# Halves in the sums behind the experts, Gelu read straight from PSUM banks, and a reordered first scan chunk

## The chip, the cores and the metric

The kernel runs on one core of one Trainium2 chip. The metric is the device time of one execution in microseconds; the value given is the median of several. Everything is float32. TensorE (PE) multiplies matrices into PSUM (eight banks of 512 columns); VectorE (DVE), ScalarE (ACT) and GpSimd (POOL) do the elementwise work; SyncE (SP) issues nearly all DMAs. GpSimd has no operand in PSUM in this kernel. Each engine takes its instructions strictly in the order in which they stand in its queue.

## The reference, cut to what matters

Input x is (4, 384, 32, 32): four batches, 384 channels, 1024 positions. Two layers follow each other, each with a mixer and a feed-forward part, both with a residual.

```python
# layer 0
x = x + L0_conv(_ln_c(x))      # selective scan over 4 directions, then layer norm and gelu
t = _to_tokens(x)              # (batch, 1024 tokens, 384)
t = t + L0_ffn(_ln_t(t))       # mixture of 4 experts, the best 2 of each token
# layer 1
x = x + L1_conv(_ln_c(x))      # attention, 8 heads of 64, one projection for q, k and v
t = t + L1_ffn(_ln_t(t))       # 384 -> 1536 -> 384 by Kronecker products, gelu between
```

```python
def step(h, inp):                                   # L0_conv, state of 16 per channel
    dA = jnp.exp(dtt[..., None] * A)
    h = h * dA + (dtt * ut)[..., None] * bt[:, :, None, :]
    y = jnp.einsum('bkdn,bkn->bkd', h, ct)
# dt = softplus(projection + bias)
# L0_ffn
h = gelu(einsum('bsd,edh->ebsh', x, w1) + b1); y = einsum('ebsh,ehd->ebsd', h, w2) + b2
out = einsum('bse,ebsd->bsd', masked, y)            # masked: renormed weights of the best two
# L1_ffn
h = gelu(x @ kron(c_fc_1, c_fc_2).T); out = h @ kron(c_proj_1, c_proj_2).T
```

## The kernel before

**The scan layer** (`scan_layer`, L186) goes through 32 units: 4 batches, 4 directions, 2 halves of 512 positions. A unit is prepared by `project` (L297), a generator that is advanced while the unit before it is scanned; the first unit has nothing before it and is prepared at once. `project` makes dt = softplus(p + bias) for three chunks of 128 channels: `begin` (L363) runs six ACT steps (Abs, Relu, Exp, +1, Ln, and 1 minus or minus 1), and the four terms ln(1+e), -e', e' and relu are then added up. For batch 0 this is done by TensorE, four products with the identity (L378, two records each); for the later batches by two GpSimd subtractions (L395, L396) and one VectorE addition (L402). Then du = dt * u is made by VectorE (L403) and dt copied by ACT (L404), and both go to DRAM (`dd`, L405, L406).

`chunk` (L409) loads dt and du back, spread over partitions as (state, channel): for each of q = 0, 1 a tile of dt (s = 0) and one of du (s = 1), each by four DMAs (L424). For each of four state groups and each q, GpSimd multiplies du by B (L440, 128x1024), ACT makes exp(A dt) (L449), VectorE scans (L454), the result is multiplied by C (GpSimd L468 for q = 0, VectorE L461 for q = 1), and TensorE adds over the states (L475).

**The tail** of a batch is put in behind the scan of the next batch and runs beside it: `route` (gates, places, rows scattered by GpSimd's indirect DMAs), `experts`, `combine`, `prologue`, `attention`, `last_layers`. The tail of the last batch, and what is left of the one before it, runs alone.

`experts` (L893) goes through 11 slots, 8 of 256 rows and 3 of 128. Per slot: TensorE fills a bank with hidden tiles (L963), ACT brings them to SBUF adding the bias (L968, Identity), and when all 12 tiles are there one wide Gelu is done in place (L971); then TensorE makes y (L978). Gelu and Exp/Ln are in different activation tables; `exp_again` (L145) loads the Exp table back at once (L148).

`combine` (L989) gathers each token's two rows by 16 indirect DMAs (L1008), adds them weighted on TensorE for each of eight blocks of 128 tokens (L1015), and VectorE adds the residual (L1018); the sum goes to DRAM in one DMA (L1019). `prologue` (L1024) then takes mean and variance of all eight blocks (`stats`, L536), the inverse root (Ln, Exp on ACT), -mean/std by `less_mean` (L548, through a "p" bank), normalises eight blocks on ACT (L1031), and transposes them to channels (L1039, copies L1043), first half before second.

`attention` (L1046) projects (L1064), transposes (L1073), and for each step multiplies scores (L1087), takes Exp (L1093) and multiplies with v (L1133).

`last_layers` (L1146) computes, for each half i, the output projection and residual (L1185, L1187), mean, variance and z (L1196 to L1216), and then the feed-forward part: `hidden` (L1224) makes six hidden tiles, two at a time: two matmuls of 32 rows (L1231), two ACT copies (L1237), and after the sixth one wide Gelu of 128x3072 (L1240) and the Exp table back. Six matmuls of 32 columns add them to f_acc (L1248). After two such groups f_acc is copied (L1253), multiplied out (L1256), added to the residual (L1258) and stored (L1259).

**Banks and buffers.** `Room` hands out tiles by tag. Beside the scan the tail has one bank "o" and three banks "p" (NARROW_BANKS); from the attention of the last batch on it has two and six (WIDE_BANKS), as the scan's banks are free.

**The order** on every queue is written when the program is built: a planner simulates the program with its own estimates of durations (`schedule_with_timeline_sim=True`, L1389) and lets each engine take the ready instruction of highest priority. Earlier emission is higher priority; `high_priority(offset=FORWARD)` moves combine, prologue and last_layers forward, and `issue_after` and `depend` tie one instruction behind another. A change in one place can so change the order elsewhere.

Of the kernel before, what the change touches and what calls it, by code (L numbers as in the profile page):

```python
# [9 lines left out]
F32 = mybir.dt.float32  # L10
I32 = mybir.dt.int32
AF = mybir.ActivationFunctionType
# [5 lines left out]
P = 128  # L18
B = 4
D = 384  # L20
DC = D // P
HW = 32
L = HW * HW
HF = 512
NH = L // HF
# [12 lines left out]
FC = HID // P  # L38
# [7 lines left out]
NSLOT = NFULL + NHALF  # L46
# [5 lines left out]
MB = L // P  # L52
# [6 lines left out]
KR = 32  # L59
# [24 lines left out]
EXACT = {"kw": 4, "k12": 2, "k4": 4, "got": 2}  # L84

FORWARD = 20000

NARROW_BANKS = {"o": 1, "p": 3}
WIDE_BANKS = {"o": 2, "p": 6}
# [26 lines left out]
class Body:  # L116
# [69 lines left out]
    def scan_layer(self, x1, between):  # L186

        nc, tc, a = self.nc, self.tc, self.a
        with ExitStack() as ctx:
# [4 lines left out]
            psum = ctx.enter_context(tc.tile_pool(name="s_ps", bufs=2, space=PSUM))  # L194
# [31 lines left out]
            def finish(b, y, i):  # L226
# [19 lines left out]
                for k in ORDER  # L246
                for i in (range(NH) if k < 2 else reversed(range(NH)))
            ]
            us = {0: start(0)}
            ahead = []  # L250
            self.place_behind = None
# [6 lines left out]
            for n, unit in enumerate(units):  # L258
                b, k, i = unit
# [37 lines left out]
    def project(self, unit, u, wx, work, dram, psum, made):  # L297
# [25 lines left out]
        def k2(name, shape=(P, HF)):  # L323
            return work.tile([*shape], F32, tag="k2", name=name, bufs=6)
# [35 lines left out]
        made += [bcs, dd]  # L360
        yield

        def begin(c):  # L363
            ps = psum.tile([P, HF], F32, tag="ps", name="dt_ps")
            nc.tensor.matmul(ps, wdt[:, c * P : (c + 1) * P], xd, start=True, stop=True)  # L365
            bias = self.col("dtb", k * DC + c)
            mag, one_e, lnw = k2("mag"), k2("one_e"), k2("lnw")
            relu = k2("relu") if b == 0 else ps
            nc.scalar.activation(mag, ps, AF.Abs, bias=bias)
            nc.scalar.activation(relu, ps, AF.Relu, bias=bias)  # L370
            nc.scalar.activation(mag, mag, AF.Exp, scale=-1.0)
# [11 lines left out]
            return ps, mag, one_e, lnw  # L383

        def behind(engine):
            if self.place_behind is None:
# [1 line left out]
            return self.tc.issue_after(self.place_behind[engine])  # L388

        for c in range(DC):  # L390
            ps, mag, one_e, lnw = begin(c)
            yield
            if b > 0:
                with behind("pool"):
                    nc.gpsimd.tensor_sub(mag, one_e, mag)  # L395
                    nc.gpsimd.tensor_sub(lnw, lnw, mag)  # L396
            yield
            d, du = mag, one_e
            rows = slice(c * P, (c + 1) * P)
            with behind("dve"):  # L400
                if b > 0:
                    nc.vector.tensor_add(ps, ps, lnw)  # L402
                nc.vector.tensor_mul(split(du), split(ps), part(c))  # L403
            nc.scalar.copy(d, ps)  # L404
            nc.sync.dma_start(out=dd[0, rows, :], in_=d)  # L405
            ins = nc.sync.dma_start(out=dd[1, rows, :], in_=du).ins  # L406
        made.append(ins)

    def chunk(self, unit, first, c, fed, carry, nega, sel, acc, work, dap):  # L409
# [6 lines left out]
        dtr = []  # L416
        for q in range(NJ // 2):

            pair = []
            at = c * P + q * 2 * DB  # L420
            for s in range(2):
                t = work.tile([P, 2, HF], F32, tag="dtr", name="dtr", bufs=7)
                for n in range(NJ):
                    nc.sync.dma_start(  # L424
                        out=t[n * DB : (n + 1) * DB],
                        in_=dd[s, at : at + 2 * DB, :].rearrange("(j d) l -> d j l", d=DB),
                    )
                pair.append(t)
            dtr.append(pair)

        def run(ap):
# [74 lines left out]
    def first_layer(self, b, room):  # L506

        self.experts(b, self.slots, room)
        with self.tc.high_priority(offset=FORWARD):
            xt, xn = self.combine(b, *self.place, room)  # L510
            return self.prologue(xt, xn, room)

    def second_layer(self, b, xc, room, between):
        att = self.attention(xc, self.sums[:, b], room)
# [18 lines left out]

        return self.x2[b].rearrange("(m p) d -> p m d", p=P)

    def stats(self, xt, eps, room):  # L536

        nc = self.nc
        st = room.tile([P, MB, 6], "st", "st")
        mv = room.tile([P, MB, 2], "mv", "mv")  # L540
        rstd = room.tile([P, MB], "rstd", "rstd")
        for m in range(MB):
            nc.vector.bn_stats(st[:, m, :], xt[:, m, :])
            nc.vector.bn_aggr(mv[:, m, :], st[:, m, :])
        self.inverse_root(rstd, mv[:, :, 1], eps)
        return mv[:, :, 0], rstd

    def less_mean(self, mean, rstd, room, tag):  # L548

        less = room.tile([P, MB], tag, "less")  # L550
        ps = room.bank("p", "less_ps")[:, :MB]
        self.nc.scalar.copy(ps, rstd)
        self.nc.vector.scalar_tensor_tensor(less, mean, -1.0, ps, op0=ALU.mult, op1=ALU.mult)
        return less
# [338 lines left out]
    def experts(self, b, routed, room):  # L893
# [60 lines left out]
        for s in range(NSLOT):  # L954
            w1, w2, bb = weights
            at, size = extent(s)
            hs = room.tile([P, FC, size], "k12", "hs")
            n = HF // size
            for f in range(0, FC, n):
                ps = room.bank("p", "h_ps").rearrange("p (r l) -> p r l", l=size)  # L960
                for r in range(n):
                    for c in range(DC):
                        nc.tensor.matmul(  # L963
                            ps[:, r, :], w1[(f + r) // wf][:, c, (f + r) % wf * P : ((f + r) % wf + 1) * P],
                            xc[:, c, :], start=(c == 0), stop=(c == DC - 1),
                        )
                for r in range(n):
                    nc.scalar.activation(  # L968
                        hs[:, f + r, :], ps[:, r, :], AF.Identity, bias=bb[:, f + r : f + r + 1]
                    )  # L970
            self.exp_again(nc.scalar.activation(hs, hs, AF.Gelu).ins)  # L971
# [12 lines left out]
            queue = nc.sync if s + 1 < NSLOT else nc.scalar  # L984
            queue.dma_start(
                out=made[at : at + size, :].rearrange("(t p) d -> p t d", p=P), in_=y
            )

    def combine(self, b, pos, gate, room):  # L989
# [22 lines left out]
        for m in range(MB):  # L1012
            ps = room.bank("p", "w_ps")[:, :D]
            for k in range(TOP):
                nc.tensor.matmul(  # L1015
                    ps, diag[k][:, m, :], got[m][:, k, :], start=(k == 0), stop=(k == TOP - 1)
                )
            nc.vector.tensor_add(xt[:, m, :], xt[:, m, :], ps)  # L1018
        nc.sync.dma_start(out=self.tokens(b), in_=xt)  # L1019
        return xt, [got[m][:, 0, :] for m in range(MB)]  # L1020

    def prologue(self, xt, xn, room):  # L1024


        nc = self.nc
        mean, rstd = self.stats(xt, self.eps6, room)
        less = self.less_mean(mean, rstd, room, "less")
        for m in range(MB):  # L1030
            nc.scalar.activation(  # L1031
                xn[m], xt[:, m, :], AF.Identity, bias=less[:, m : m + 1], scale=rstd[:, m : m + 1]
            )
        xc = room.tile([P, DC, L], "k12", "xc")
# [111 lines left out]
    def last_layers(self, b, att, room, between=()):  # L1146
# [72 lines left out]

        for step in between:  # L1220
            step()
        ng = 6

        def hidden(i, at):  # L1224
            hs = room.tile([P, ng, HF], "k12", "hs")
            early = None
            for f in range(at, at + ng, 2):
# [269 lines left out]
```

## Time and profile before

| what | value |
|---|---|
| median of 3 runs (lowest, highest) | 4267.21 us (4253.81, 4271.01) |
| the profiled execution | 4260.96 us |
| its span, first to last instruction | 4258.3 us |
| busy: PE, POOL, DVE, ACT | 3330.8, 3020.0, 2838.3, 2519.7 us |
| granted TensorE clock, mean | 0.873 of full |

Where the time lies: the first product of the scan on GpSimd starts at 44.08 us; the first experts at 864; the scan's last accumulation ends at about 3426. The last batch's experts end at 3939, its gathers and sums at 3968, its attention at 4143, and its last output leaves VectorE at 4251.69.

How to read it: a line of the order of time gives start, length, engine, line, operation, output and inputs, shape and count; in brackets stands how long the engine was idle before it and what released it. Consecutive instructions of one kind are merged into one line, whose length then reaches from the first start to the last end. A float32 matmul appears as two records. A list of waits gives who waited, for whom, us in all, times, the longest. "Granted clock" is the share of TensorE's full clock that the throttle allowed.

### The profile page before, as it was taken

What the parts mean: (1) busy time and instruction counts of PE and PEld (TensorE: products, weight loads), DVE (VectorE), ACT (ScalarE), POOL (GpSimd) and SP (SyncE); (2) the same over time, 40 slices, a digit from 0 to 9 for tenths busy, and PEclk for the clock granted to TensorE, in tenths of its full rate; (3) what the DMA queues carried; (4) which work ended last, traced back from release to release, by engine and by line L of the source; (5) the groups of instructions that cost most, each with busy time, mean ns of one, the idle gap of its engine ahead of it and who ended that gap; (6) DMA issues with size and microseconds to landing.
All of it is one profiled execution on the core that took longest, in us unless ns stands there. A gap on an engine that the chain in (4) does not pass through costs nothing. (4 is left out here: it accounts for less than half of the span.)

```text
span 4258.3 us, 45670 instructions
## 1 busy us (share of the span) xinstructions
PE 3330.8 (78%) x13308; PEld 1572.8 (37%) x13308; DVE 2838.3 (67%) x4148; ACT 2519.7 (59%) x4486; POOL 3020.0 (71%) x1471
## 2 busy tenths in 40 slices
PE   6445544389887888689996888679986899998896
PEld 2111101155553223255552223245553235666222
DVE  5999997788877877788877878778877830000101
ACT  5555545566665876666665776667664763443454
POOL 5999998898888977889989888879988830000100
PEclk8766666699998999699998999689997999999997
DMA  5554464678786534668887434668788343345100
GB/s 140 126 129 122 124 172 110 204 204 233 228 257 162 152 107 136 192 204 230 232 258 210 124 100 133 192 183 235 225 250 230 93 152 110 121 150 191 50 26 20
DMA packets 410322, 693.70 MB, mean 163 GB/s; under 512 B 51024, under 2 KB 209616, under 8 KB 410064
## 3 DMA queue, kind: packets, MB, share of 16 engines
q1 hardware_dynamic: 400752, 664.29, 54.3%
q0 software_dynamic: 8192, 25.17, 1.8%
q8 instruction: 107, 1.75, 0.2%
q14 instruction: 151, 1.24, 0.1%
q10 hardware_dynamic: 1120, 1.25, 0.1%
HBM read 569.00 MB, written 121.50 MB: 162 GB/s over the span
## 5 line engine op out<-in xcount | busy, mean ns | idle before, releaser
L440 POOL TENSOR_TENSOR bx<-dtr,bcs 128x1024 f32<-128x1024 f32 x768 | 1793.7, 2362 | 195.6 <-PE acc L475 84.0
L449 ACT ACTIVATE da<-dtr,nega 128x512 f32<-128x512 f32 x1536 | 1045.9, 690 | 898.8 <-DVE bx L461 551.1
L468 POOL TENSOR_TENSOR bx<-bx,bcs 128x1024 f32<-128x1024 f32 x384 | 905.4, 2362 | 132.4 <-DVE carry L465 59.9
L475 PE MATMUL acc<-bx,sel 128*32 128x512 f32 x3072 | 488.0, 691 | 309.8 <-POOL bx L468 282.2
L963 PE MATMUL h_ps<-xc,w 128*128 128x256 f32 (+1 forms) x3168 | 666.6, 365 | 65.6 <-DVE xc L950 28.3
L978 PE MATMUL y_ps<-w,hs 128*128 128x384 f32 x1824 | 643.7, 506 | 55.9 <-ACT hs L971 54.9
L963 PEld LDWEIGHTS h_ps<-xc,w 128*128 128x128 f32 x3168 | 551.9, 198 | 241.3 <-issue 124.5
L454 DVE TENSOR_TENSOR_SCAN bx<-da,carry,bx 128x512 f32<-128x512 f32 x384 | 473.7, 1271 | 134.5 <-POOL bx L440 69.5
L454 DVE TENSOR_TENSOR_SCAN bx<-da,bx 128x512 f32<-128x512 f32 x384 | 452.3, 1210 | 125.4 <-POOL bx L440 69.7
L454 DVE TENSOR_TENSOR_SCAN da<-da,carry,bx 128x512 f32<-128x512 f32 x384 | 475.7, 1274 | 79.5 <-ACT da L449 63.1
L461 DVE TENSOR_TENSOR bx<-da,bcs 128x512 f32<-128x512 f32 x768 | 509.6, 681 | 2.9
L454 DVE TENSOR_TENSOR_SCAN da<-da,bx 128x512 f32<-128x512 f32 x384 | 455.4, 1219 | 67.5 <-ACT da L449 46.8
L978 PEld LDWEIGHTS y_ps<-w,hs 128*128 128x128 f32 x1824 | 353.1, 197 | 338.5 <-issue 68.7
L1093 ACT ACTIVATE ex<-s_ps 128x512 f32<-128x512 f32 x512 | 300.2, 591 | 128.7 <-PE s_ps L1087 126.8
L1087 PE MATMUL s_ps<-w 64*128 64x512 f32 x1024 | 302.6, 653 | 70.1 <-ACT ex L1093 68.4
L968 ACT ACTIVATE hs<-h_ps,bb 128x256 f32<-128x256 f32 (+1 forms) x528 | 199.4, 441 | 220.0 <-PE h_ps L963 216.4
L999 POOL TENSOR_TENSOR diag<-ident,g_weight 128x1024 f32<-128x1024 f32 x8 | 15.0, 1898 | 419.9 <-PE xc_ps L946 406.4
L1133 PE MATMUL o_acc<-ex,vt 128*64 128x512 f32 x1024 | 281.9, 629 | 18.3 <-ACT ex L1093 14.7
L475 PEld LDWEIGHTS acc<-bx,sel 128*32 128x32 f32 x3072 | 75.0, 115 | 597.1 <-POOL bx L468 392.5
L982 DVE TENSOR_TENSOR y<-y_ps,bb 128x384 f32<-128x384 f32 x76 | 41.8, 550 | 223.4 <-PE y_ps L978 223.2
L1087 PEld LDWEIGHTS s_ps<-w 64*128 64x128 f32 x1024 | 80.6, 187 | 271.4 <-ACT ex L1093 222.7
L365 PE MATMUL dt_ps<-xd,wdt 108*128 108x512 f32 x192 | 123.7, 731 | 69.6 <-ACT mag L404 37.0
(213 smaller groups left out, 3611.4 us busy)
## 6 DMA issues: line engine op xcount, KB each, us to landing
w<-in_w SPq DMA_DIRECT2D x352, 576.0 KB
dtr<-dd SPq DMA_DIRECT2D x1536, 128.0 KB
bcs<-both SPq DMA_DIRECT2D x512, 128.0 KB
dd<-one_e SPq DMA_DIRECT2D x96, 256.0 KB
dd<-mag SPq DMA_DIRECT2D x96, 256.0 KB
rows<-zero SPq DMA_DIRECT2D x76, 192.0 KB
xt<-x SPq DMA_DIRECT2D x32, 384.0 KB
xs<-rows SPq DMA_DIRECT2D x32, 384.0 KB
```

Source lines behind the costliest of these rows:

```text
L440: pool = nc.gpsimd.tensor_mul(bx, dtr[q][1], bc[:, 0].unsqueeze(1).to_broadcast([P, 2, HF])).ins
L449: nc.scalar.activation(da, dtr[q][0][:, j, :], AF.Exp, scale=nega[:, col : col + 1])
L454: nc.vector.tensor_tensor_scan(run(h), run(da), run(bx[:, j, :]), 0.0 if first else hold, ALU.mult, ALU.add,)
L461: dve = nc.vector.tensor_mul(bx[:, j, :], h, cg).ins
L468: pool = nc.gpsimd.tensor_mul(bx, bx, cg.unsqueeze(1).to_broadcast([P, 2, HF])).ins
L475: nc.tensor.matmul(acc[lo : lo + DB, :], sel, out[q][:, j, :], start=(g == 0), stop=(g == NG - 1),)
L963: nc.tensor.matmul(ps[:, r, :], w1[(f + r) // wf][:, c, (f + r) % wf * P : ((f + r) % wf + 1) * P], xc[:, c, :], start=(c == 0), stop=(c = ...
L968: nc.scalar.activation(hs[:, f + r, :], ps[:, r, :], AF.Identity, bias=bb[:, f + r : f + r + 1])
L978: nc.tensor.matmul(out[:, :D], hs[:, f, t * P : (t + 1) * P], w2[f // wf][:, f % wf, :], start=(f == 0), stop=(f == FC - 1),)
L1087: ins = nc.tensor.matmul(ps, w[rows, j * P : (j + 1) * P], w[rows, halves(i)], start=True, stop=True).ins
L1093: done.append(nc.scalar.activation(ex[:, o, :], ps, AF.Exp, scale=HD**-0.5, accum_out=sums[:, t, 2 * j + o, i : i + 1],).ins)
L1133: ins = nc.tensor.matmul(out[cols, :], made[t][1][:, j, cols], ex[:, o, :], start=(j == 0), stop=(j == MB - 1),).ins
```

## The change

Seven edits, in the order of the program:

1. Five (`WARM = 5`) matmuls of `ones` with itself (128x512) stand ahead of the first unit; nobody reads their result.
2. In the first unit, for its first chunk alone, dt is added up by GpSimd and VectorE, as in later batches, instead of by TensorE; Relu then stays in the bank.
3. For that chunk `chunk` loads du's tile ahead of dt's.
4. In the last slot of `experts` (128 rows, three banks of four tiles) the first eight tiles get one wide Gelu, tied behind the first matmul of the last tile; the last four tiles get Gelu with the bias straight from the bank.
5. The sums of `combine` become a function that `prologue` calls block by block; the store to DRAM goes in two halves.
6. `prologue` does statistics, inverse root, normalisation and transposes half by half; the "less" value goes through an "o" bank.
7. In the last batch `hidden` is replaced by `quickly`: four hidden tiles in four "p" banks, four Gelus straight from the banks, no copy, no `exp_again`; three such groups of four for each half instead of two of six.

```diff
+            warm = psum.tile([P, HF], F32, tag="ps", name="warm")
+            for _ in range(WARM):
+                nc.tensor.matmul(warm, self.ones, self.ones.unsqueeze(1).to_broadcast([P, HF // P, P]),
+                    start=True, stop=True)
             us = {0: start(0)}
...
+        alone = len(self.kept) == 1
         def begin(c):
+            by_products = b == 0 and not (alone and c == 0)
...
-            relu = k2("relu") if b == 0 else ps
+            relu = k2("relu") if by_products else ps
...
-            if b == 0:
+            if by_products:
...
-            if b > 0:
+            if not by_products:
                 with behind("pool"):
                     nc.gpsimd.tensor_sub(mag, one_e, mag)
...
-            for s in range(2):
+            for s in (1, 0) if unit == (0, 0, 0) and c == 0 else (0, 1):
```

```diff
             for f in range(0, FC, n):
+                last = s == NSLOT - 1 and f == FC - n
...
+                        if last and r == n - 1 and c == 0:
+                            wide = nc.scalar.activation(hs[:, :f, :], hs[:, :f, :], AF.Gelu).ins
+                            self.depend(wide, ins)
                 for r in range(n):
-                    nc.scalar.activation(
-                        hs[:, f + r, :], ps[:, r, :], AF.Identity, bias=bb[:, f + r : f + r + 1]
-                    )
-            self.exp_again(nc.scalar.activation(hs, hs, AF.Gelu).ins)
+                    done = nc.scalar.activation(
+                        hs[:, f + r, :], ps[:, r, :], AF.Gelu if last else AF.Identity,
+                        bias=bb[:, f + r : f + r + 1],
+                    ).ins
+            if not last:
+                done = nc.scalar.activation(hs, hs, AF.Gelu).ins
+            self.exp_again(done)
```

```diff
-        for m in range(MB):
+        def add(m):
...
-        nc.sync.dma_start(out=self.tokens(b), in_=xt)
+            if m % (MB // NH) == MB // NH - 1:
+                part = slice(m + 1 - MB // NH, m + 1)
+                nc.sync.dma_start(out=self.tokens(b)[:, part, :], in_=xt[:, part, :])
...
         for i in range(NH):
+            for j in range(nh):
+                m = i * nh + j
+                add(m)
+                nc.vector.bn_stats(st[:, j, :], xt[:, m, :])
+                nc.vector.bn_aggr(mv[:, j, :], st[:, j, :])
+            self.inverse_root(rstd, mv[:, :, 1], self.eps6)
+            less = self.less_mean(mv[:, :, 0], rstd, room, f"less{i}", "o")
+            for j in range(nh):
+                m = i * nh + j
+                nc.scalar.activation(
+                    xn[m], xt[:, m, :], AF.Identity, bias=less[:, j : j + 1], scale=rstd[:, j : j + 1]
+                )
             for c in range(DC):
                 ps = room.bank("p", "tc_ps")
```

```diff
-        ng = 6
+        alone = room.banks is WIDE_BANKS
+        ng = nq if alone else 6
+        def quickly(i, at):
+            hs = room.tile([P, ng, HF], "k12", "hs")
+            banks = [room.bank("p", "h_ps") for _ in range(nq)]
+            for o, ps in enumerate(banks):
+                rows = slice(o * KR, (o + 1) * KR)
+                nc.tensor.matmul(ps, fc1[rows, at // nq, :], zs[i][rows, :], start=True, stop=True)
+            for o, ps in enumerate(banks):
+                nc.scalar.activation(hs[:, o, :], ps, AF.Gelu)
+            return hs
```

More of the change, by code (lines that the diff above doesn't have):

```diff
@@ L86 @@
 FORWARD = 20000
+WARM = 5
 NARROW_BANKS = {"o": 1, "p": 3}
@@ L248, in scan_layer @@
             ]
+            warm = psum.tile([P, HF], F32, tag="ps", name="warm")
+            for _ in range(WARM):
+                nc.tensor.matmul(
+                    warm, self.ones, self.ones.unsqueeze(1).to_broadcast([P, HF // P, P]),
+                    start=True, stop=True,
+                )
             us = {0: start(0)}
@@ L382, in begin @@
                 nc.scalar.activation(one_e, one_e, AF.Identity, bias=self.minus1)
-            return ps, mag, one_e, lnw
+            return by_products, ps, mag, one_e, lnw
         def behind(engine):
@@ L390, in project @@
         for c in range(DC):
-            ps, mag, one_e, lnw = begin(c)
+            by_products, ps, mag, one_e, lnw = begin(c)
             yield
-            if b > 0:
+            if not by_products:
                 with behind("pool"):
@@ L400, in project @@
             with behind("dve"):
-                if b > 0:
+                if not by_products:
                     nc.vector.tensor_add(ps, ps, lnw)
@@ L417, in chunk @@
         for q in range(NJ // 2):
-            pair = []
+            pair = [None, None]
             at = c * P + q * 2 * DB
-            for s in range(2):
+            for s in (1, 0) if unit == (0, 0, 0) and c == 0 else (0, 1):
                 t = work.tile([P, 2, HF], F32, tag="dtr", name="dtr", bufs=7)
@@ L427, in chunk @@
                     )
-                pair.append(t)
+                pair[s] = t
             dtr.append(pair)
@@ L509, in first_layer @@
         with self.tc.high_priority(offset=FORWARD):
-            xt, xn = self.combine(b, *self.place, room)
-            return self.prologue(xt, xn, room)
+            xt, xn, add = self.combine(b, *self.place, room)
+            return self.prologue(xt, xn, room, add)
     def second_layer(self, b, xc, room, between):
@@ L534, in tokens, with less_mean @@
         return self.x2[b].rearrange("(m p) d -> p m d", p=P)
[L536 to L541, printed above, removed]
-        for m in range(MB):
[L543 to L551, printed above, removed]
+    def less_mean(self, mean, rstd, room, tag, bank="p"):
+        n = rstd.shape[-1]
+        less = room.tile([P, n], tag, "less")
+        ps = room.bank(bank, "less_ps")[:, :n]
         self.nc.scalar.copy(ps, rstd)
@@ L962, in experts @@
                     for c in range(DC):
[L963 removed]
+                        ins = nc.tensor.matmul(
                             ps[:, r, :], w1[(f + r) // wf][:, c, (f + r) % wf * P : ((f + r) % wf + 1) * P],
                             xc[:, c, :], start=(c == 0), stop=(c == DC - 1),
[L966 removed]
+                        ).ins
+                        if last and r == n - 1 and c == 0:
+                            wide = nc.scalar.activation(hs[:, :f, :], hs[:, :f, :], AF.Gelu).ins
+                            self.depend(wide, ins)
                 for r in range(n):
[L968 to L971 removed]
+                    done = nc.scalar.activation(
+                        hs[:, f + r, :], ps[:, r, :], AF.Gelu if last else AF.Identity,
+                        bias=bb[:, f + r : f + r + 1],
+                    ).ins
+            if not last:
+                done = nc.scalar.activation(hs, hs, AF.Gelu).ins
+            self.exp_again(done)
             if s + 1 < NSLOT:
@@ L1011, in combine @@
                 )
-        for m in range(MB):
+        def add(m):
             ps = room.bank("p", "w_ps")[:, :D]
@@ L1018, in combine, with prologue @@
             nc.vector.tensor_add(xt[:, m, :], xt[:, m, :], ps)
-        nc.sync.dma_start(out=self.tokens(b), in_=xt)
-        return xt, [got[m][:, 0, :] for m in range(MB)]
-    def prologue(self, xt, xn, room):
-        nc = self.nc
[L1028 to L1034, printed above, removed]
-        for i in range(NH):
+            if m % (MB // NH) == MB // NH - 1:
+                part = slice(m + 1 - MB // NH, m + 1)
+                nc.sync.dma_start(out=self.tokens(b)[:, part, :], in_=xt[:, part, :])
+        return xt, [got[m][:, 0, :] for m in range(MB)], add
+    def prologue(self, xt, xn, room, add=lambda m: None):
+        nc = self.nc
+        nh = MB // NH
+        xc = None
+        for i in range(NH):
+            st = room.tile([P, nh, 6], f"st{i}", "st")
+            mv = room.tile([P, nh, 2], f"mv{i}", "mv")
+            rstd = room.tile([P, nh], f"rstd{i}", "rstd")
+            for j in range(nh):
[9 more added lines that the diff above has]
+                    xn[m], xt[:, m, :], AF.Identity, bias=less[:, j : j + 1], scale=rstd[:, j : j + 1]
+                )
+            if xc is None:
+                xc = room.tile([P, DC, L], "k12", "xc")
             for c in range(DC):
@@ L1221, in last_layers @@
             step()
-        ng = 6
+        alone = room.banks is WIDE_BANKS
[5 more added lines that the diff above has]
+                rows = slice(o * KR, (o + 1) * KR)
+                nc.tensor.matmul(
+                    ps, fc1[rows, at // nq, :], zs[i][rows, :], start=True, stop=True
+                )
+            for o, ps in enumerate(banks):
+                nc.scalar.activation(hs[:, o, :], ps, AF.Gelu)
+            return hs
         def hidden(i, at):
+            if alone:
+                return quickly(i, at)
             hs = room.tile([P, ng, HF], "k12", "hs")
```

## The prediction

> **What bounds it now.** I read the table of stages first (busy time of each engine between two times; columns: stretch, its length, busy us and count for PE, PEld, DVE, ACT, POOL, then the granted TensorE clock, DMA share, GB/s).
>
> ```profile
> 44.00:864.00 820.00, 392.95 (x1234) 111.59 (x1234) 719.32 (x1034) 433.22 (x677) 775.00 (x353) 0.67 0.53 141
> 864.00:3428.00 2564.00, 2157.19 (x8989) 1065.65 (x8989) 2025.24 (x2876) 1707.07 (x3035) 2205.05 (x1067) 0.91 0.66 189
> 3428.00:3942.00 514.00, 488.23 (x2023) 294.04 (x2021) 56.23 (x151) 214.93 (x398) 23.06 (x21) 0.98 0.45 150
> ...
> 4193.00:4252.00 59.00, 33.07 (x102) 8.26 (x98) 5.81 (x10) 32.27 (x33) 0.00 (x0) 0.65 0.06 22
> ```
>
> The scan alone is GpSimd's (775 of 820 us); the scan beside the other work is shared between GpSimd (86%) and TensorE (84%); from 3428 on TensorE is the limit (95%, and 98% in the attention up to 4143). In the last 59 us nobody is: PE 56%, ACT 55%, and the clock falls to 0.65. A stage that no engine fills is a chain of waits, so next I read who TensorE waits for there:
>
> ```profile
> PE f_acc L1248 <- ACT hs L1240: 20.9, 4, 5.2
> ```
>
> Four waits of 5.2 us, one for each group of six hidden tiles. ScalarE's own order of time shows what is in one:
>
> ```profile
> 4193.94 1.07 ACT L1237 COPY hs<-h_ps 128x512 f32<-128x512 f32 x2 [0.72 <-PE h_ps L1231]
> 4195.03 1.28 ACT L1240 ACT_TABLE_LOAD   x1
> 4196.33 2.76 ACT L1240 ACTIVATE hs<-hs 128x3072 f32<-128x3072 f32 x1
> 4199.11 1.28 ACT L148 ACT_TABLE_LOAD   x1
> ```
>
> The last copy, a table load, the wide Gelu, a load back: nothing of f_acc can start before 4199.1.
>
> **Gelu from the banks (quickly, last batch only).** Removed: 24 copies (12.9 us busy), four wide Gelus (11.0), eight table loads (10.3; four of them before a Gelu). Added: 24 Gelus of 128x512, one load. No row has Gelu at this size. The two widths of L971/L1240 give it: (2.764 - 1.483) us for 1536 more columns is 0.834 ns a column, and 0.20 us is fixed, so 0.63 us alone; two copies of 0.58 take 1.07, so neighbours start 0.49 apart. 24 Gelus are then 11.8 to 15.1 us; I take 13.2. *ACT's bound:* z of the second half ends on ACT at 4192.26, load 1.28, 13.2: 4206.7. If the planner puts the first four Gelus ahead of that z (h_ps is ready at 4188.96), ACT fills its idle time but pays one more load in each direction, 2.6 us: about the same end. *PE's bound:* a round of four tiles is h_ps x8, 1.14 us, and eight f_acc records at 3.55/12, 2.4 us (half clock): six rounds 21.2, and the first half's fo_ps 4.95: 26.1 from 4187.8, plus x_var 2.0: 4215.9. After the last round comes what came before: now from the last Gelu (4241.57) to the last out (4251.69) is 10.1 us, of which 3.6 f_acc. Behind ACT's bound 10.1 less 1.2 to 2.6: 4214.9. Behind PE's bound fy, fo_ps and out, 6.4: 4222.3, less where the clock is full (h_ps at 4204.42 is; PE will no longer stand for 5.2 us). I take 4218, so **-33.5**. Ends: -38 (ACT's bound, full clock) and -21 (half clock all through, with waits for banks: six "p" banks, four held by a round).
>
> Here the Trainium skill (ScalarE: Activation LUTs, "What ACT_TABLE_LOAD costs") differs from the trace: it puts a drain of about 1.38 us behind every load of 1.28. In the rows above the Gelu starts 1.30 after the load starts, so no drain is seen; by the page an extra pair of loads would cost 5.3 instead of 2.6 us, and the removal would bring that much more. The rows decide.
>
> **Halves in the sums and the prologue.** In batch 3 all of this is exposed:
>
> ```profile
> 3967.34 0.55 DVE L1018 TENSOR_TENSOR xt<-xt,w_ps 128x384 f32<-128x384 f32 x1 [1.17 <-PE w_ps L1015]
> ...
> 3969.77 4.89 ACT L1031 ACTIVATE got<-xt,less,rstd 128x384 f32<-128x384 f32 x8 [0.28 <-DVE less L553]
> ...
> 3976.63 5.32 PE L1064 MATMUL w_ps<-xc,wqkv 128*128 128x512 f32 x12
> ```
>
> The gathers (16 on POOL, 1.26 us apart, to 3964.2) set when the last sum comes; that stays. Behind it now stand eight normalisations and the copies of both halves. With halves only four stand there (-2.45), and 12 of the 24 transposes, three copies and the first half's w_ps (2.66) go into PE's waits for gathers (11.7 us). The second half's w_ps, now at about 3979.2, would start at 3972.2 (fourth normalisation) + 0.4 + three copies, 1.6: 3974.2. **-5**; ends -2.4 (the planner leaves w_ps behind) and -8 (scores of the first half slip in as well). The second set of Ln, Exp, copy, less (0.84 us) lies behind the gathers; without that cover it costs 0.84. The store in two halves is one more issue of 0.39 on SP, which is idle from 3968.3 to 3982. The moved less bank ("o" for "p") is free between y_ps and o_acc.
>
> **Last slot.** Now:
>
> ```profile
> 3925.50 1.14 ACT L968 ACTIVATE hs<-h_ps,bb 128x128 f32<-128x128 f32 x4 [1.54 <-PE h_ps L963]
> 3926.66 1.28 ACT L971 ACT_TABLE_LOAD   x1
> 3927.95 1.48 ACT L971 ACTIVATE hs<-hs 128x1536 f32<-128x1536 f32 x1
> ```
>
> and y_ps starts at 3929.49 after a 4.0 us wait. The wide Gelu is now 1024 columns, 1.06 us, and waits for a matmul about 0.5 us before the bank is done (3924.95). If the load is not held by that wait: load at 3923.96, wide to 3926.3, then four small ones in 1.14, to 3927.5. If it is: 3928.5. y_ps can start with the first eight tiles after the wide one and PE stands 1 to 2 us instead of 4.0, so its 9.65 may become the 7.91 of the slot before. **-3**; ends 0 and -4.5. What queues behind the waiting Gelu on ACT is in this batch only the four small ones; in batches 0 to 2 it is the scan's da (L449), for which DVE and then POOL wait, and a da between the wide Gelu and the small ones costs two loads: 2.6 us three times at most, no gain taken.
>
> **Head.**
>
> ```profile
> 32.62 0.69 DVE L403 TENSOR_TENSOR one_e<-dt_ps,u 128x512 f32<-128x512 f32 x1 [13.93 <-issue]
> ...
> 37.56 5.49 SPq L424 DMA_DIRECT2D dtr<-dd  x12
> ...
> 44.08 2.35 POOL L440 TENSOR_TENSOR bx<-dtr,bcs 128x1024 f32<-128x1024 f32 x1 [41.89 <-DMA dtr<-dd]
> ```
>
> The eight identity matmuls end at 32.52. Instead: the last ACT step ends at 27.67, two POOL subtractions at 1.27 (L395, L396), a DVE add of 0.69: 30.9, so du is 1.7 earlier. POOL is idle there. du's four loads come first, 2.4 sooner (d landed at 41.68, du at 44.08): POOL starts near 40.0, 4.1 earlier. But d now lands second, at about 42.4, and its Exp (0.69) ends at 43.1: the first scan moves from 46.46 to 43.1. **-3**; ends 0 and -5.5. From 44 to 864 POOL is full, so this shifts everything. Chunks 1 and 2 gain nothing: a chunk keeps POOL for 12 x 2.36 us.
>
> WARM is five matmuls, ten records of 0.9 at the half clock of ln_mean (5.40 for six): from 1.1 (ones is set) to 10.1, where ln_mean now starts at 5.71; at ln_var's 2.84 for six it would then end at 12.9 instead of 11.1: +1.8. If the clock rises on the way, they end near 7.9 and ln_mean at 10.7: -0.4, and -2.1 if xd_ps (4.52 for six) keeps that clock too. Taken as 0, within the ends above.
>
> The Trainium skill (TensorE: Matmul & The Clock Gate, "Part 1: The HAM clock gate") says that about 3.4 us of work raises the clock and that it is checked in free-running windows. By it I estimate a gain of 1 us; xd_ps at 17.54, at half clock after 2.15 us of idling, speaks for little lasting beyond that.
>
> **Sum.** -33.5 - 5 - 3 - 3 = -44.5 on the profiled execution, 4260.96 us (span 4258.3 and 2.7 around it): **4216**. That execution lies 6 us under the median of the three runs, 4267.21, whose own spread is 17; a measurement of this kernel can tell about 0.5% (21 us) from no change, so faster means under 4246, slower over 4288. The unmeasured term is the rest of the scan: the planner writes every queue anew, and a first chunk of other operations changes its times. The nearest rows are single waits in 850 to 3420: up to 18.9 us (PE for POOL's bx), 20.8 (POOL, issue). I take 0 and one such wait either way: +20, -20.
>
> **Rivals.**
> - *The end is paced by PE at half clock and by banks* (9.9 of the 33.1 us of PE work there are fo_ps at 0.83 a record): the end keeps half its gain, 16: 4234. For: the clock of 0.65. Against: the 5.2 us gaps that drop it go. 0.17.
> - *The new plan of the scan gives most of it back*: two of those 18.9 us waits on PE or POOL, which are both about 85% full: 4216 + 38 = 4254, no change. 0.12.
> - *The new plan helps* (the 115 us in which y_ps waits for hs, and 85 for gathers, shrink in batches 0 to 2 too): 4196. 0.09.
> - *Slower*: POOL's queue in the scan. POOL's product waits now 328 us in all (195.6 + 132.4 at L440, L468). If the new order puts products behind late carries and accs, it decides from +51 us on (16%), where the time is the old median, and passes 4288 at +72 (22%); at +33% (108) it is 4324. For: 84 of these us are waits for PE's acc, and PE's order is rewritten. Against: the loop's instructions are the same but for one chunk of 96. 0.06.
> - That the fast path isn't taken can't be: its test is the bank table of the last batch.
>
> Forecast 0.56 (own range 4204 to 4230). Faster: 0.56 + 0.17 + 0.09 = 0.82; same 0.12; slower 0.06. The range runs from the helpful plan, 4196, to 4252, half way through the second rival.
>
> **What would show it.** Right: L1240 without wide Gelus, f_acc's wait of 20.9 under 8, the last out near 26 us after the second half's z leaves ACT (now 59); w_ps of L1064 starting before the last sum; first POOL product near 40; the scan's last product 3 us sooner. Wrong: granted clock under 0.7 in the last stretch with PE full; a scan end that has moved by more than 10 us either way, which would be the planner and not an edit.

## The result, and the profile after

The changed kernel takes 4262.11 us (median of 14 runs, 4253.12 to 4271.85), the kernel before 4264.4 beside it: ratio 0.9997, 95% interval 0.9988 to 1.0006. No change, where 4216 was forecast and 4196 to 4252 was the range. Its profiled execution took 4253.12 us (span 4251.4), 7.84 less than the one of before; it is the fastest of the 14, and the medians lie only 2.3 apart. Line numbers have moved: GpSimd's products are now L450, the C products L478, da L459, acc L485, w_ps of the sums L1021, the Gelu from banks L1256, f_acc L1285, out L1295.

The table of stages after (columns as in the prediction):

```profile
44.00:864.00 820.00, 390.38 (x1212) 112.19 (x1210) 709.41 (x1016) 428.18 (x671) 752.92 (x342) 0.68 0.49 135
...
4193.00:4252.00 59.00, 48.96 (x155) 15.59 (x153) 8.96 (x15) 23.05 (x36) 0.00 (x0) 0.95 0.08 28
```

The last stretch went as hoped: clock 0.95 instead of 0.65, TensorE 49 us busy instead of 33. But in the first stretch, which no edit was meant to touch beyond its first 12 products, GpSimd gets 752.9 us of work done where it did 775.0: 22 us of its work are pushed out.

Where the 7 us of the span come from is read by following the same milestone through both traces (after minus before, us; a product is one of GpSimd's multiplications with du, counted from 0, and from the second row on a milestone is an end):

| milestone | prediction | measured |
|---|---|---|
| first product on GpSimd | -4.1 | -4.7 |
| product 63 (270 us before) | -3 | +11.6 |
| product 191 (749 us), end of batch 0 | -3 | +17.6 |
| last product of the scan (3418 us) | -3 | +22.7 |
| last y of the experts | -6 | +16.5 |
| end of the last attention | -11 | +15.7 |
| last out leaves VectorE | -44.5 | -7.0 |

From the attention's end to the last out 22.7 us are won; 22.7 are lost by the end of the scan. (Between the two 7.0 come back. The last slot has some 2.5 of that, as e5 below shows, and the halves 0.8; batch 2's tail, which TensorE works off behind the scan, has its last out 20 us sooner than before.) How far such milestones can be trusted: e3 and e5 below keep the scan's order of before, and still differ from it by up to 2.0 at product 191, 6.0 at product 383, the end of batch 1, and 1.1 at the scan's end. Who GpSimd waits for in 44 to 864, first before, then after:

```profile
POOL bx L468 <- DVE carry L465: 12.3, 5, 4.9
POOL bx L440 <- PE acc L475: 10.3, 2, 9.9
```

```profile
POOL bx L450 <- PE acc L485: 31.8, 7, 10.8
POOL bx L478 <- DVE carry L475: 14.2, 7, 5.2
```

A product waits for PE's acc when all six bx buffers hold something that TensorE has not yet summed. That wait has tripled, by 21.5 us, about what is lost. The reason lies in the order of GpSimd's queue (d: products with du, L440/L450; b: C products; how many in a row). Before, this is the rhythm of most of batch 0; after, it is how the queue begins:

```
before  d3 b1 d2 b1 d2 b1 d1 b1  d3 b1 d2 b1 d2 b1 d1 b1 ...
after   d6 b3 d6 b3 d5 b2 d1 b1  d6 b3 d6 b3 d6 b3 d5 b2 d1 b1 ...
```

Before, batch 0 has 2 runs of six products; after, 14. Six products fill all six buffers, and the next can only come when the oldest of them has been scanned, multiplied by C, and summed. GpSimd's order of time after shows such runs:

```profile
69.32 13.90 POOL L450 TENSOR_TENSOR bx<-dtr,bcs 128x1024 f32<-128x1024 f32 x6 [3.08 <-PE acc L485]
83.16 4.66 POOL L478 TENSOR_TENSOR bx<-bx,bcs 128x1024 f32<-128x1024 f32 x2
88.90 2.35 POOL L478 TENSOR_TENSOR bx<-bx,bcs 128x1024 f32<-128x1024 f32 x1 [1.08 <-DVE carry L475]
93.48 11.60 POOL L450 TENSOR_TENSOR bx<-dtr,bcs 128x1024 f32<-128x1024 f32 x5 [2.23 <-PE acc L485]
```

Of the seven waits for acc six stand directly behind six products and three C products, 21.0 us in all. The seventh, 10.8 at 702, has nothing to do with runs: it is there before too (9.9 at 683).

### The profile page after: what moved, and what is told of

Same layout as the page of the kernel before. It is cut to its first block, busy times and chain, and to the rows that moved or that the text cites. A ratio compares the mean times of both kernels' runs of the same rounds, so it can differ in the third digit from the quotient of the medians.

```text
span 4251.4 us, 45715 instructions
## 1 busy us (share of the span) xinstructions
PE 3335.4 (78%) x13310; PEld 1578.0 (37%) x13310; DVE 2845.2 (67%) x4153; ACT 2504.6 (59%) x4492; POOL 3022.2 (71%) x1473
## 5 line engine op out<-in xcount | busy, mean ns | idle before, releaser
L450 POOL TENSOR_TENSOR bx<-dtr,bcs 128x1024 f32<-128x1024 f32 x768 | 1790.9, 2360 | 182.8 <-PE acc L485 132.0
L459 ACT ACTIVATE da<-dtr,nega 128x512 f32<-128x512 f32 x1536 | 1045.2, 690 | 952.3 <-DVE bx L471 589.2
L478 POOL TENSOR_TENSOR bx<-bx,bcs 128x1024 f32<-128x1024 f32 x384 | 903.0, 2359 | 127.9 <-DVE carry L475 70.6
L485 PE MATMUL acc<-bx,sel 128*32 128x512 f32 x3072 | 492.0, 694 | 310.9 <-POOL bx L478 268.8
L1108 PE MATMUL s_ps<-w 64*128 64x512 f32 x1024 | 311.5, 656 | 59.0 <-ACT ex L1114 55.4
L1154 PE MATMUL o_acc<-ex,vt 128*64 128x512 f32 x1024 | 286.7, 637 | 25.1 <-ACT ex L1114 19.2
L485 PEld LDWEIGHTS acc<-bx,sel 128*32 128x32 f32 x3072 | 77.0, 115 | 606.3 <-POOL bx L478 363.9
```

What stands on the lines that cost most here:

```text
L450: pool = nc.gpsimd.tensor_mul(bx, dtr[q][1], bc[:, 0].unsqueeze(1).to_broadcast([P, 2, HF])).ins
L459: nc.scalar.activation(da, dtr[q][0][:, j, :], AF.Exp, scale=nega[:, col : col + 1])
L478: pool = nc.gpsimd.tensor_mul(bx, bx, cg.unsqueeze(1).to_broadcast([P, 2, HF])).ins
L485: nc.tensor.matmul(acc[lo : lo + DB, :], sel, out[q][:, j, :], start=(g == 0), stop=(g == NG - 1),)
L1108: ins = nc.tensor.matmul(ps, w[rows, j * P : (j + 1) * P], w[rows, halves(i)], start=True, stop=True).ins
L1154: ins = nc.tensor.matmul(out[cols, :], made[t][1][:, j, cols], ex[:, o, :], start=(j == 0), stop=(j == MB - 1),).ins
```

## The experiments

The theory at the start: each edit is worth about what it was forecast, but the order planned at build changes all through the scan with any edit, and costs what the end gains. The rival: the end itself gains less. "Product 191" is the end of batch 0's scan, as above.

**Tail alone, head alone, one edit alone.** e1 is the change without its head:

```
-WARM = 5
-by_products = b == 0 and not (alone and c == 0)
+by_products = b == 0
-for s in (1, 0) if unit == (0, 0, 0) and c == 0 else (0, 1):
+for s in (0, 1):
```

> Edits 4 to 7 alone; the first chunk and everything ahead of it as before, so GpSimd's order of products in batch 0 is the old one. Theory (the changed order on GpSimd in batch 0, six products of du and then three of C, costs about 20 us there, and the end brings its gain): the scan of batch 0 ends as before, the end brings about 26 us, the last slot and the halves 1 to 3, a new plan of batches 1 to 3 within 10 either way: about 4235 us, 4225 to 4245. Rival (the scan is lost to edits 4 to 6 in the tails of batches 0 to 2): about 4264, no change. Rival (the end's gain is eaten by something in the end itself): about 4264 too, with no stretch that is 26 us shorter.

Measured: 4277.83, ratio 1.0024 [1.0012, 1.0036] (95% interval), above all that was expected. e2 is the head alone (the old experts, sums, prologue and end).

> Edits 1 to 3 alone (five idle matmuls, the first chunk summed by GpSimd, its du first); the tail is the old one. Theory (GpSimd's order in batch 0): slower by 18 to 30 us, 4282 to 4294, nearly all of it lost between 50 and 500 us. Rival (the head is worth its 4 us and the loss comes from the tail's edits): 4260.

Measured: 4292.7, 1.0065 [1.0047, 1.0083], as the theory had it. First product -4.5, product 191 +17.7, scan's end +24.4. In e1 batch 0 keeps its order (product 191 -3.6), and batches 1 to 3 lose: scan's end +27.7. So either half loses the scan some 25 us, at different places. e3 is the Gelu from banks alone (head as in e1, `last = False`, the old sums and prologue).

> Edit 7 alone (Gelu from banks in the last batch's feed-forward part). GpSimd's order in the whole scan is the old one. Theory: the scan is untouched, and the last stretch is shorter by about 26 us: 4238, 4234 to 4244. Rival (the end gives nothing by itself): 4264.

Measured: 4244.74, 0.9952 [0.9933, 0.997]. Its scan keeps the old order (product 191 and the scan's end within 1.2 us), and from the attention's end (+1.2) to the last out (-20.5) the end gains 21.7, where 26 was expected: that is the clean worth of this edit.

**The other tail edits.** e6 is the last slot's Gelu alone, e7 the halves alone.

> Edit 4 alone, in all batches. With edits 4 to 7 together the scan and the tail of batch 2 lost some 40 us. Theory a (it is edit 4: a Gelu tied behind a matmul on ACT's queue in the scan): 4285 to 4300. Theory b (it is the halves): 4255 to 4268. Theory c (neither by itself; any edit in the tail makes another plan, and its luck is anything within 30 us): anything, with gains or losses at places where the edit is not.

> Edits 5 and 6 alone, in all batches. Theory a: 4255 to 4268. Theory b (the halves cost the 40 us): 4285 to 4305. Theory c as for the last slot.

Measured: e6 4272.79, 1.0012 [0.9999, 1.0025], scan's end +19.2; e7 4262.04, 0.9994 [0.998, 1.0008], scan's end -5.5 and batch 2's tail +24. Neither costs the 40 by itself, so theory c, another plan with every edit, is what is left. Both are in all four batches, and in batches 0 to 2 their instructions stand in the queues of the scan. e5 keeps all tail edits, but these two in the last batch only, where no scan runs beside them:

```
-last = s == NSLOT - 1 and f == FC - n
+last = b == B - 1 and s == NSLOT - 1 and f == FC - n
 ...
+if b < B - 1:
+    xt, xn = self.combine_whole(b, *self.place, room)
+    return self.prologue_whole(xt, xn, room)
```

> Edits 4 to 7, but edits 4 to 6 for batch 3 alone; batches 0 to 2 and the head as before. The order of the scan's instructions is then the old one up to the end of the scan. Theory (the edits are worth what they do in the exposed tail, and what was lost in the run with edits 4 to 7 in all batches was lost to a new order of the scan in batches 1 to 3): 25 from Gelu out of banks, 2.4 from the last slot, 1 to 5 from the halves: 4236, 4229 to 4242. Rival (edits 4 to 6 are slow in the last tail itself): 4250 to 4278.

Measured: 4239.57, 0.9938 [0.9921, 0.9955]. The scan is that of before (its end +0.9), the last y comes 2.5 sooner, the attention's end 3.2, the last out 24.8. So the last slot is worth 2.5 (3.4 counted from the scan's end), the halves 0.7, and Gelu from the banks 21.6. The time is in the expected range.

**The head.** e4 is the change without the idle matmuls (`WARM`).

> The changed kernel without the five idle matmuls. GpSimd's order in batch 0 has 21 runs of six products instead of 14 in the changed kernel and 2 in the one before. Theory (the runs of six are what costs): batch 0 loses about 30 us instead of 20, so about 4272, 4266 to 4280. Rival (order is not the cause; the matmuls are worth under 2 us either way): 4262, 4259 to 4265.

Measured: 4277.99, 1.0031 [1.0018, 1.0045]; product 191 +22.4 with 21 runs of six: not the idle matmuls. e8 has these matmuls, the sum on GpSimd and the Gelu from banks, but du loaded second, as before; its order has 2 runs of six.

> Edits 1, 2 and 7: idle matmuls, the first chunk summed by GpSimd, Gelu from banks; du is not loaded first. GpSimd's order in batch 0 then has two runs of six products, as before, not 14. Theory (the runs of six cost the 18 to 20 us of batch 0): product 191, which starts at 749 us in the kernel before and 17.7 later with edits 1 to 3, starts between 4 earlier and 2 later; the time is near that of edit 7 alone, 4243, plus or minus 15 for the plan of batches 1 to 3. Rival (the sum on GpSimd or the idle matmuls cost it): product 191 is 15 or more later, 4260 to 4268.

Measured: 4266.8, 1.0004 [0.9992, 1.0015]. Product 191 is at -4.1: batch 0 loses nothing; but batches 1 to 3 have another plan again, scan's end +15.6, and the time is where the rival had it.

**Are the runs of six the cause, or company?** e9 is the change and one line in every chunk, which puts a group's second product behind the C product of the group before; e10 the same on e5.

```
+if q == 1 and behind_c is not None:
+    self.depend(pool, behind_c)
```

> The changed kernel, with one line of order added on GpSimd for every unit: the second product of a state group (q = 1) stands behind the C product of the group before it. Nothing is computed differently. Runs of six products are gone from batch 0 (14 before; now none over five). Theory (the runs of six cost batch 0 its 18 to 20 us): product 191 goes from 17.6 later than in the kernel before to between 6 earlier and 3 later; in all about 4242, with 15 either way for the new plan of batches 1 to 3. Rival (the runs only accompany a loss that the head's edits cause otherwise): product 191 stays 12 or more later.

> Edits 4 to 7 with 4 to 6 for batch 3 alone, the old head, and the same added line of order. Theory: batch 0 had hardly any runs of six, so product 191 stays within 3 us; batches 1 to 3 have two runs of six each less; 4239, with 12 either way. If runs of six in batches 1 to 3 cost much, 4225 to 4232. Rival (the added line costs by itself, each wait some 20 ns or a worse order): batch 0 later by 5 or more, 4248 or more.

Measured: 4351.07, 1.0204 [1.0186, 1.0222], product 191 +74.3; and 4372.69, 1.0252 [1.0232, 1.0271], +67.6. Both theories missed. The traces say why: with no run of six (e9) or one (e10) the du products' wait for acc in 44 to 864 is small, 14.2 and 11.2, but C products now wait 68.4 and 71.1 us for VectorE, where they waited 14.3 before. So the line takes the one wait away and brings a larger one; order alone moves batch 0 by 70 us. e13 and e14 are gentler: the change, and one wait for one instruction of the first chunk of all, at group 2 and, with `g in (1,)`, at group 1.

```
+if unit == (0, 0, 0) and c in (0,) and g in (2,) and q == 0:
+    self.depend(pool, done_c[g - 1])
```

> All seven edits, and one more line of order: in the very first chunk alone, the first product of group 2 goes behind group 1's C product. It binds a single instruction near 50 us; written out, GpSimd's order of batch 0 then has 1 run of six products where the change has 14, and returns to the old rhythm of three, two, two and one. Theory (runs of six, which fill all six bx buffers so that the next product waits for acc on PE, cost batch 0 its 20 us): product 191 at -8 to 0 against before, where the change stood at +17.6. Rival (the runs only accompany; the sum on GpSimd or du's early load costs it otherwise): product 191 stays at +12 or more. In both, batches 1 to 3 are planned anew, so the whole is only bounded: 4225 to 4290.

> The same line one group earlier (the first product of group 1 behind group 0's C product). Written out, batch 0 now has 20 runs of six and 9 of five, where the change has 14 and 6. Theory: product 191 at +22 to +38, in proportion to the runs. Rival (runs only accompany): as the change, +14 to +20; and if the line itself costs, e13, with the same line, loses as much. The whole is bounded by the replanned batches 1 to 3: 4255 to 4310.

| kernel | runs of six in batch 0 | GpSimd's wait for acc, 44 to 864 | GpSimd busy there | product 191 |
|---|---|---|---|---|
| before | 2 | 10.3 | 775.0 | 0 |
| e13 | 1 | 13.0 | 774.7 | -7.7 |
| after | 14 | 31.8 | 752.9 | +17.6 |
| e14 | 20 | 27.6 | 748.1 | +24.1 |

The waits of GpSimd in e13, then in e14 ("issue" is a stretch that the profile gives no releaser for):

```profile
POOL bx L451 <- PE acc L489: 13.0, 3, 10.1
...
POOL bx L481 <- DVE carry L478: 8.5, 3, 4.9
```

```profile
POOL bx L451 <- PE acc L489: 27.6, 9, 4.5
POOL bx L481 <- DVE carry L478: 16.7, 9, 4.9
POOL bx L451 <- issue: 10.8, 1, 10.8
```

The 10.8 of "issue" in e14 lies at 708, where the other three wait for acc for about 10 us. Without that place the wait for acc is 0.4 and 2.9 in the two with few runs, 21.0 and 27.6 in the two with many: about what product 191 loses. The same edits with the runs gone are 25 us faster there than with them, and with more runs slower, both as expected: the order with runs of six is the cause of batch 0's loss. What the head's own edits are worth is not settled by this: e15 below has e13's order in batch 0 and stands at -3.9, e1 with the old head at -3.6. As a whole e13 takes 4327.71, 1.0095 [1.0065, 1.0125], outside what was expected (its batches 1 to 3 lose 71 us from product 191 to the scan's end), and e14 4293.5, 1.0012 [1.0, 1.0023]. (e13 to e16 ran where the kernel before takes 4289.9; the ratios are to that, but the milestones are still against the trace of before that is kept. e16 against e11, which have equal queues in the scan, gives what that does to them: 1.0 at product 191, 4.3 at the scan's end.)

**Keeping the parts that pay.** e11 is e5 with the sum on GpSimd for the first chunk, e12 e5 with du first, e15 e5 with the whole head and e13's wait.

> Edits 4 to 7 with 4 to 6 for batch 3 alone, and of the head only edit 2 (first chunk summed by GpSimd). No runs of six in batch 0 but one. Theory: product 191 between 4 earlier and 1 later; batches 1 to 3 get a new plan (six runs of six in batch 1 instead of two), so 4239 plus 0 to 20. Rival (edit 2 by itself costs batch 0 ten or more).

> Edits 4 to 7 with 4 to 6 for batch 3 alone, and of the head only edit 3 (du first). Two runs of six in batch 0. Theory: product 191 between 4 earlier and 2 later; a new plan of batches 1 to 3 (six and three runs of six), so 4239 plus 0 to 20. Rival (edit 3 by itself costs batch 0 ten or more).

> Halves, and the Gelu in the last slot, in the last batch alone; Gelu from banks; the whole head; and the line of e13, so that batch 0 has one run of six. Theory: the end's 25 and the head's 4 are kept, product 191 at -8 to 0; batches 1 to 3 have a plan of their own again, worth -10 to +30 by e6, e8 and e11. So 4264 - 28 - 4 = 4232, 4222 to 4262. Rival (whichever head is taken costs 15 or more by the plan of batches 1 to 3, and e11 was the lucky one): above 4250.

Measured: e11 4225.24, 0.9904 [0.9886, 0.9923], scan's end -4.7, better than expected; e12 4272.36, 1.0017 [1.0005, 1.0028], product 191 -1.7 but scan's end +19.8, worse than expected; e15 4283.1, 0.9977 [0.9967, 0.9987], product 191 -3.9, scan's end +24.5. For e15 the rival came true: each other head gave batches 1 to 3 another plan, and among e8, e11, e12, e13 and e15 only e11's did not lose. Nothing in its one edit says why, so it counts as luck of the plan.

**What paces the end now.** e16 is e11 with the Gelus in groups of three and two lines of order, one for h_ps (behind the last Gelu of the group before the last) and one for f_acc (behind the last Gelu of its own group); its order up to there is that of e11.

```
-ng = nq if alone else 6
+ng = 3 if alone else 6
 ...
+    if len(turns) > 1:
+        self.depend(ins, turns[-2])
 ...
+if alone:
+    self.depend(ins, turns[-1])
```

> e11 with the end's Gelus taken in groups of three tiles instead of four, and two lines of order: a group's h_ps go behind the last Gelu of the group before the last, a group's f_acc behind its own last Gelu. Of six banks three are then always free for the next group, and PE gets its h_ps and f_acc in blocks instead of one by one; the order of the scan is that of e11. Theory (in the change PE, which alternates single h_ps and f_acc at 2.04 us a tile, paces the end, since tiles in other row groups would run beside each other): the stretch from the second half's z on DVE to the last out falls from 33.7 us to 22 to 27, with the Gelus 0.5 us apart, and the whole to 4217, 4208 to 4226, 0.988. Rival (ACT or the loads of its table pace the end): 32 to 35 us, and the time of e11, 4225.

Measured: **4234.0 where before takes 4289.9: 0.9865 [0.984, 0.9889]**, the lowest ratio of all, though its interval meets e11's, and the time is above the 4208 to 4226 expected, which was reckoned from 4264. The stretch that was edited says more: from the second half's z on ScalarE to the last out it takes 26.9 us, where the change took 33.7 and e11 34.9: the upper end of the theory's 22 to 27, and not the rival's 32 to 35. TensorE's order of time in a piece of the end, after:

```profile
4203.57 1.14 PE L1252 MATMUL h_ps<-z,wc 32*128 32x512 f32 x8
...
4209.56 1.12 PE L1252 MATMUL h_ps<-z,wc 32*128 32x512 f32 x2
4210.61 1.04 PE L1285 MATMUL f_acc<-hs,wc 128*32 128x512 f32 x2
4211.58 1.12 PE L1252 MATMUL h_ps<-z,wc 32*128 32x512 f32 x2
4212.63 1.05 PE L1285 MATMUL f_acc<-hs,wc 128*32 128x512 f32 x2
```

and in e16:

```profile
4220.04 1.13 PE L1319 MATMUL h_ps<-z,wc 32*128 32x512 f32 x6
4221.10 1.06 PE L1355 MATMUL f_acc<-hs,wc 128*32 128x512 f32 x6
4222.09 1.13 PE L1319 MATMUL h_ps<-z,wc 32*128 32x512 f32 x6
4223.16 1.06 PE L1355 MATMUL f_acc<-hs,wc 128*32 128x512 f32 x6
```

A tile is two records. Four tiles take 1.14 us, three 1.13, and one alone 1.12: tiles on different rows of the array run beside each other, and one alone costs as much as four. In the change a group holds four of six banks, so the next group's h_ps come one by one, as banks are freed, each between two f_acc: 2.03 us a tile. In e16 three tiles take 2.05. Whether the groups of three would do without the two lines of order is not shown.

## Why the prediction was wrong, point by point

- **The failed step is "the rest of the scan": taken as 0, with ±20 by the size of single waits.** The planner did write every queue anew, and that was worth +25.7 at the scan's last product (-3 forecast, +22.7 measured): 20.6 of it by the end of batch 0, where the runs of six are, and 5.1 in batches 1 to 3, where the cause stays open. It is the second rival, "the new plan of the scan gives most of it back", that came; it had been given 0.12. Its mechanism was half right: not two waits of 18.9, but six of 2.2 to 4.4 for acc behind runs of six, 21.0 in all. The fourth rival had named that wait (84 of GpSimd's us are for PE's acc); what was missing is that a burst of one kind of product, as long as there are buffers, makes it. Gelu from the banks and the halves were mis-sized as well, by 10.8 and 4.2.
- **Gelu from banks, -33.5:** the right edit and mechanism, mis-sized: 21.7 alone, 22.7 in the change. The first rival had half the gain by PE at half clock and by banks; the clock rose to 0.95, but PE did pace the end, by banks and so by single tiles. I had costed a round of four tiles at 1.14 us for h_ps x8 and 2.4 for f_acc, 3.5 in all; taken one by one, four tiles are four times 2.03, 8.1. And the early Gelus cost more than "one more load in each direction". ScalarE after:

```profile
4203.67 1.28 ACT L1256 ACT_TABLE_LOAD   x1
4204.97 2.07 ACT L1256 ACTIVATE hs<-h_ps 128x512 f32<-128x512 f32 x4
4207.05 1.28 ACT L153 ACT_TABLE_LOAD   x1
4208.35 0.69 ACT L153 ACTIVATE z<-x_var,eps 128x512 f32<-128x512 f32 x1
4209.05 1.28 ACT L154 ACT_TABLE_LOAD   x1
4210.35 0.63 ACT L154 ACTIVATE z<-z 128x512 f32<-128x512 f32 x1
4210.99 1.28 ACT L1256 ACT_TABLE_LOAD   x1
```

  Three more loads than a run of Gelus needs, 3.84 us, and z is 3.0 us later against the attention's end. The Gelus were sized well: 0.52 each in a row of four, 0.55 assumed.
- **Halves, -5:** right in place, wrong in TensorE's queue: 0.7 in e5, 0.8 in the change. The low end named for it, -2.4 with w_ps left behind, is what the planner wrote: the first half's w_ps too starts only at 3991.06, behind the last sum. TensorE after, behind the fourth sum:

```profile
3972.68 0.91 PE L1021 MATMUL w_ps<-got,diag 128*128 128x384 f32 x2 [0.30 <-DMA got<-made,g_pos]
3976.82 2.82 PE L1060 MATMUL tc_ps<-ident,got 128*128 128x128 f32 x12 [3.23 <-ACT got L1052]
3979.89 5.48 PE L1021 MATMUL w_ps<-got,diag 128*128 128x384 f32 x16 [0.25 <-ACT xc L1064]
3988.57 1.64 PE L1060 MATMUL tc_ps<-ident,got 128*128 128x128 f32 x8 [3.20 <-ACT got L1052]
```

  The first half's transposes stand ahead of the second half's sums, so PE stops 3.2 us for a normalisation while the second half's first rows come in, and 3.2 once more for the second half. On VectorE the last sum ends 6.3 us behind the start of the last gather, where it was 4.6 before: 1.7 of the 2.4 are lost again. I had the transposes fill waits for gathers, and the reverse happened.
- **Last slot, -3:** right. 2.5 to 3.4 in e5; in the change y_ps waits 2.04 instead of 4.0 and takes 8.01 instead of 9.65. The table load was held by the wait for the matmul, the later of the two cases named:

```profile
3945.27 1.28 ACT L968 ACT_TABLE_LOAD   x1 [1.14 <-PE h_ps L963]
3946.57 1.06 ACT L968 ACTIVATE hs<-hs 128x1024 f32<-128x1024 f32 x1
```

- **Head, -3:** the first product came 4.7 sooner (at 39.42), where 4.1 had been worked out, but that is in part luck. du's load ahead of dt's gave 2.1 of the 2.4 counted, and the sum on GpSimd 0.9 of the 1.7; the other 1.7 is xd_ps, at 2.83 us instead of 4.52, a gain of the idle matmuls that had been weighed and put at 0. All seven executions with these matmuls have xd_ps at 2.83, but so have three of eleven without them (e1, e4, e10), so it is not theirs alone. By its own order the head cost 17.6 at product 191. That order needs the sum and du's load together: e8 has the one and e12 the other, and neither has more than two runs.

What stays open: which property of a plan makes batches 1 to 3 lose 15 to 70 us. In e1, e4, e8, e12 and e15 batch 2's experts come 30 to 60 us late; in e1 between 2750 and 3000 the experts get 288 records of h_ps instead of 360, and f_acc of batch 1's end has 48 there instead of 24, so batch 1's end has slipped into the place of the next batch's experts. That is seen, not tried.

## What to carry to other kernels

Where queues are written by a planner, an edit at the end is not local: compare the written order of the bottleneck engine before trusting a sum, and put the edit only where no other stage shares the queues (e5 against the change: about the same gain at the end, 21.6 and 22.7, and 23 us better as a whole). Bursts as long as a buffer pool turn an elastic queue into a wait; three products in a row were better than six here, and e9's order, in twos and fours with the C products early, was worse than both. And give small matmuls on row groups in blocks: halve the group before letting the next one come in single tiles.

## What the runs showed of the hardware

- A 32-row tile alone took 1.12 us on TensorE, four in a row 1.14, and a change between h_ps (32 rows by 128 columns) and f_acc (128 by 32) came every 0.97 to 1.07 us. The Trainium skill (TensorEngine Tiling (Array Packing), "Key Properties") has both halves of that: tiles work in parallel, and a change of the tiling mode drains the engine. The trace agrees with the first; no run separates the drain.
- Ln and Exp behind a Gelu each loaded a table (4207.05 and 4209.05 above). The Trainium skill (ScalarE: Activation LUTs, "Table sets: the hidden batching unit") counts one load for Ln and then Exp, from a set that holds both. Here it is two; the kernel before, which loads a set by hand behind each Gelu (L148), runs the z steps with none between them. The measurement decides: put the load in by hand.
- Equal queues can take unequal time. From 3450 to 3600, e11 and then e16, whose queues are equal there:

```profile
3450.00:3600.00 150.00, 145.73 (x637) 73.16 (x634) 22.78 (x91) 69.71 (x179) 15.58 (x16) 0.99 0.49 167
```

```profile
3450.00:3600.00 150.00, 135.72 (x572) 66.03 (x572) 21.57 (x90) 65.50 (x175) 15.58 (x16) 0.92 0.47 160
```

  The granted clock is 0.92 instead of 0.99, and TensorE is busy for 10 us less; e16's scan ends 4.3 later than e11's, its batch 2's z 18.8 later. Whether the clock fell first or TensorE waited first is not shown. Nor is it the chip alone: on chip 11 the kernel before took 4263.63 beside e5 to e8 and 4289.9 beside e13 to e15. Ratios to the kernel before, run alongside, and not times, are what these comparisons rest on.
